# A four-layer convolution block on one core: the order of the start, of the spectra stage, of the attention weights, and fill products in the output stage

## The chip, the cores and the metric

The kernel runs on one core of a Trainium2 chip. The metric is device time in microseconds (us) of one execution. One profiled execution gives the trace that is read here; its rows give starts and durations, with the source line of the kernel.

The engines are TensorE (PE, with its weight loads shown apart as PEld), VectorE (DVE), ScalarE (ACT), GpSimd (POOL) and SyncE (SP), which issues most DMAs. [...]

## The reference, cut to what matters

Input x is (4, 56, 56, 128) in float32. Four layers follow each other, each with a residual and a group norm without weights in front of it:

```python
x = x + L0(_gn(x))   # shifted-window attention, global attention, MLP (per sample)
x = x + L1(_gn(x))   # all pairs of nodes in a row: relu(proj_i + proj_j), summed, then a linear
x = x + L2(_gn(x))   # spectral (FFT) convolutions, attention over the 56 images, two more spectral layers
x = x + L3(_gn(x))   # 3x1 convolution, sums over both axes, relu
```

In layer 2 each sample's 56 images are normalised, transformed by `rfft2`, multiplied by complex weights per head (32 heads) for K, Q and V, scored image against image, softmaxed, and mixed; then come projection, two spectral layers with norms, and the residuals.

## The kernel before, in words

All transforms are products with constant matrices. The stages, in order of time:

1. **Start** (to 48 us): `input_norms` loads the four samples and their norms, and computes a bound on the attention scores, which decides by a branch on the chip (`z_small`) whether the fast layers may be used. Python generators interleave the steps by hand: `norm_steps` for each sample, `products` (squared lengths) and `longest` (their maxima), `weights` (which runs `score_bounds`, `attention_bias` and `edge_weights`). `fill(n)` issues n products of ones whose result nobody reads.
2. **Layers 0 and 1** (48 to 2586.5 us): a loop over the four samples, `fast_layer` and then `edge_layer`. The normalised images of samples 0 to 2 (`xad`, and transposed `xat`) are written to DRAM by `normed_images` beside the next sample's work; sample 3 stays in `x1` in SBUF, and is normalised in the next stage.
3. **Spectra** (to 2671.3 us): `first_transform` (4 blocks `s_pr` of 28 products a sample, scaled by VectorE into `s_z` and copied by ScalarE) and `sample_spectra` (13 steps: three `s_ps`, two `s_pr2`, eight `s_px`, copied into S, iS, R and xh). `norm` is sample 3's `normed_images`, advanced by `go_on(n)`. Beside it POOL prepares the weights of the scores (`all_score_weights`) and of the values (`value_weights`, which ends in the DRAM tensor `dd`).
4. **Attention weights** (to 2801.6 us): `attention_weights` runs 72 items: for each of two pairs of samples (bp) and 16 columns c, one with n=0 (the operand `q_u` made by VectorE, 128x1792) and one with n=1 (made by POOL), and four odd ones per pair that read T and Tp. `make` issues an operand four items ahead, `product` the eight products of an item. `between` holds generators that get a step after each item: `skips`, and, when pair 0 is done, its `softmax`. `collect` adds a pair's sums.
5. **Attend** (to 3122.8 us): `attend` multiplies xh by `dd`'s values (VectorE `u_ud`, POOL `u_up`) and sums with the attention in `u_po`; pair 1's softmax is among its first steps.
6. **Outputs** (to the end): `outputs` records 788 operations in a `Plan`, and issues them in a fixed order, `OUTPUT_ORDER`. `bank` and `banks` hand out PSUM.

TensorE, ScalarE and VectorE run in the order of the program text in these stages (a manual schedule), POOL too from stage 4 on; SP's DMAs, and POOL's work before that, are placed by the framework's scheduler.

## Time and profile before

| | us |
|---|---|
| median of 3 runs | 3463.82 |
| lowest, highest | 3462.63, 3465.51 |
| profiled execution | 3464.84 |
| its span, first to last instruction | 3463.1 |

Busy time of the engines by stage, from one answer for these six stretches (us):

| stage | length | PE | DVE | ACT | POOL | mean granted clock |
|---|---|---|---|---|---|---|
| start | 48.0 | 27.28 | 29.72 | 16.32 | 7.95 | 0.92 |
| layers 0 and 1 | 2538.5 | 2460.57 | 1989.59 | 1862.21 | 648.89 | 1.00 |
| spectra | 84.8 | 77.21 | 39.98 | 32.72 | 39.72 | 0.96 |
| attention weights | 130.3 | 123.06 | 94.33 | 7.04 | 99.76 | 0.96 |
| attend | 321.2 | 316.49 | 277.84 | 68.49 | 267.01 | 0.99 |
| outputs | 340.2 | 314.41 | 226.41 | 144.36 | 222.59 | 0.98 |

The granted clock is TensorE's, as a share of full speed. A TensorE that is busy at half clock counts as busy, so the column PE and the clock are read together.

### The profile page before, as it was taken

Reading aid. Unit: us, or ns where it says so; the run is one execution under the profiler, and the core shown is the slowest. Engines: PE = TensorE matmul, PEld = TensorE weight load, DVE = VectorE, ACT = ScalarE, POOL = GpSimd, SP = SyncE. Lnnn points to the kernel's source line nnn. Section 1 sums busy time; section 2 is a strip of 40 time slices with the busy share of each in tenths; the row PEclk is TensorE's granted clock in tenths of the full one; section 3 lists DMA queues with packets and bytes.
Section 4 is the critical chain, followed back from the end, with each engine's and each line's share of the span. In section 5 each row is a group of like instructions: output and inputs, shape, how many; then the busy total and the mean of one; then the engine's idle time right before and its main releaser. Section 6 shows DMA issues by size and latency. Waiting matters only on the chain. (4 is left out here: it accounts for less than half of the span.)

```text
span 3463.1 us, 64456 instructions
## 1 busy us (share of the span) xinstructions
PE 3319.0 (96%) x27800; PEld 1425.6 (41%) x27800; DVE 2657.9 (77%) x2555; ACT 2131.1 (62%) x2253; POOL 1285.9 (37%) x796
## 2 busy tenths in 40 slices
PE   7999999999999999999999999999999999999998
PEld 4433333353333435333343443333337433336664
DVE  6588867867888696788859858887794778895776
ACT  4688876668888575788857668887653012215442
POOL 1000007800000491000019400000775778884786
PEclk9999999999999999999999999999999999999999
DMA  2143420024434000444310033442014037743101
GB/s 106 43 94 89 97 54 19 20 53 93 92 91 86 19 1 20 106 103 91 91 42 1 20 81 90 93 97 54 1 40 118 1 87 187 190 115 94 57 20 56
DMA packets 98012, 243.41 MB, mean 70 GB/s; under 512 B 64457, under 2 KB 69833, under 8 KB 92713
## 3 DMA queue, kind: packets, MB, share of 16 engines
q0 software_dynamic: 16128, 102.77, 14.8%
q1 hardware_dynamic: 74872, 123.61, 12.2%
q10 hardware_dynamic: 6720, 12.85, 1.3%
q8 instruction: 220, 3.60, 0.4%
q14 instruction: 72, 0.58, 0.1%
HBM read 79.43 MB, written 31.33 MB: 32 GB/s over the span
## 5 line engine op out<-in xcount | busy, mean ns | idle before, releaser
L830 ACT ACTIVATE f_ring<-f_pm 128x1792 f32<-128x1792 f32 (+1 forms) x764 | 1093.8, 1482 | 226.4 <-PE f_pm L827 179.6
L682 DVE TENSOR_TENSOR f_acc<-f_acc,f_ring 128x1792 f32<-128x1792 f32 x468 | 947.5, 2025 | 190.2 <-ACT f_ring L830 160.0
L827 PE MATMUL f_pm<-f_qT,f_kT 32*128 32x448 f32 x5376 | 722.6, 571 | 9.9 <-ACT f_p L716 4.1
L672 POOL DMA_DIRECT2D f_far<-f_ring x112 | 96.5, 862 | 1328.2 <-ACT f_ring L830 1033.4
L693 PE MATMUL f_pm<-f_ring,f_va 128*32 128x448 f32 (+1 forms) x6304 | 589.4, 490 | 0.0
L1269 POOL TENSOR_TENSOR e_tp<-e_a,e_c 128x1792 f32<-128x1792 f32 (+2 forms) x172 | 480.4, 2831 | 36.7 <-issue 36.7
L1267 DVE TENSOR_TENSOR e_td<-e_a,e_pc 128x1792 f32<-128x1792 f32 (+2 forms) x292 | 478.3, 1703 | 8.8 <-ACT e_c L1255 8.8
L827 PEld LDWEIGHTS f_pm<-f_qT,f_kT 32*128 32x128 f32 x5376 | 260.2, 183 | 411.5 <-ACT f_ring L830 300.3
L693 PEld LDWEIGHTS f_pm<-f_ring,f_va 128*32 128x32 f32 x6304 | 163.8, 109 | 410.1 <-issue 397.8
L1271 ACT ACTIVATE e_tp<-e_tp 128x1792 f32<-128x1792 f32 (+2 forms) x172 | 253.3, 1495 | 98.0 <-POOL e_tp L1269 98.0
L2018 DVE TENSOR_TENSOR u_ud<-u_px,u_d 112x1792 f32<-112x1792 f32 x144 | 263.4, 1863 | 39.7 <-PE u_po L2023 35.1
L2020 POOL TENSOR_TENSOR u_up<-xh,u_d 112x1792 f32<-112x1792 f32 (+1 forms) x72 | 240.9, 3373 | 55.0 <-PE u_po L2023 40.7
L1338 PE MATMUL e_acc<-e_td,t_edge 128*32 128x448 f32 x1952 | 231.6, 542 | 6.6 <-DVE e_td L1267 6.4
L2023 PE MATMUL u_po<-u_ud,AT 112*64 112x448 f32 x1056 | 213.9, 544 | 1.9 <-DVE u_ud L2018 1.9
L1338 PE MATMUL e_acc<-e_tp,t_edge 128*32 128x448 f32 x1184 | 147.9, 543 | 23.7 <-ACT e_tp L1271 23.7
L2023 PEld LDWEIGHTS u_po<-u_ud,AT 112*64 112x64 f32 x1056 | 74.3, 138 | 128.9 <-issue 112.8
L1338 PEld LDWEIGHTS e_acc<-e_td,t_edge 128*32 128x32 f32 x1952 | 61.6, 110 | 142.6 <-issue 93.7
L737 DVE RECIPROCAL f_den<-f_den 128x448 f32<-128x448 f32 x28 | 82.6, 2951 | 44.9 <-ACT f_den L734 44.9
L1862 POOL TENSOR_TENSOR q_u<-iS,q_g 128x1792 f32<-128x1792 f32 x32 | 102.8, 3235 | 22.8 <-PE q_acc L1877 22.8
L813 POOL TENSOR_TENSOR x<-xf,xw 128x343 f32<-128x343 f32 x28 | 25.5, 911 | 224.7 <-DVE xf L802 224.7
L1877 PE MATMUL q_acc<-q_u,S 64*64 64x448 f32 x1024 | 104.4, 552 | 4.4 <-DVE q_u L1864 3.3
L2121 ACT COPY x_ev<-x_po 56x896 f32<-56x896 f32 x32 | 28.8, 900 | 126.9 <-DMA x_xs<-xat 51.1
(525 smaller groups left out, 4579.1 us busy)
## 6 DMA issues: line engine op xcount, KB each, us to landing
f_far<-f_ring POOLq DMA_DIRECT2D x112, 896.0 KB, 6.4
u_d<-dd SPq DMA_DIRECT2D x46, 784.0 KB
f_far<-f_ring SPq DMA_DIRECT2D x28, 896.0 KB
xw<-in_x SPq DMA_DIRECT2D x4, 1568.0 KB
x2d<-x SPq DMA_DIRECT2D x4, 1568.0 KB
xat<-x SPq DMA_DIRECT2D x4, 1568.0 KB
x_xs<-xat ACTq DMA_DIRECT2D x32, 196.0 KB
xm<-x_ev ACTq DMA_DIRECT2D x64, 98.0 KB
```

Of the source, the lines that this page charges most:

```text
L682: nc.vector.tensor_add(e.acc, e.acc, slots(j, c))
L693: nc.tensor.matmul(e.po[heads[h], part], va[o, c, heads[h]], p, start=(c == 0), stop=(c == 23 and part.stop == NB))
L827: nc.tensor.matmul(ss[:, i, :NB], kT[heads[h], c * P:(c + 1) * P], qT[heads[h], blk(j)], start=True, stop=True)
L830: nc.scalar.activation(ring[:, slot:slot + m, :], ss[:, :m, :NB], AF.Exp, scale=scale)
L1267: nc.vector.tensor_tensor(t, am, cm, ALU.max)
L1269: nc.gpsimd.tensor_sub(t, am, cm)
L1271: nc.scalar.activation(tf, tf, AF.Relu)
L1338: nc.tensor.matmul(acc[quarters[r0 + r], :NB], w.S[:, 0, :], t[:, r].rearrange("p l n -> p (l n)"), start=(g == 0), stop=(g == len(turns) ...
L1877: nc.tensor.matmul(acc[bp][i][halves[hb % 2], hb // 2, :NB], x[o], u[o, 8 * hb:8 * hb + 8, :].rearrange("p h t -> p (h t)"), start=first, ...
L2018: nc.vector.tensor_mul(u, bc(px[:, :, :NB], 2, m), dm)
L2020: nc.gpsimd.tensor_mul(u, bc(x, 2, m), dm)
L2023: nc.tensor.matmul(po[64 * b2:64 * b2 + 64, :NB], st.AT[:, 8 * i + h0 + q, 2 * bp + b2, :], u[:, b2, q, :], start=(left == 16), stop=(left ...
```

## The change

- **Start.** The bias products and sums (`attention_bias`) go ahead of the last sample's norm; one fill of two is dropped; the lengths of sample 2 are reduced ahead of that sample's last norm step; the sums of the bounds go under the transpose of the maxima.
- **Spectra.** The buffer `xw` moves from the io pool to the right side of memory, and with one more row it also holds images. Image 0 is read into it (`first_image`) when the last sample's front has used it, so during the last edge layer; image 2 is read into it later; the images' pool has one buffer instead of two. All four transform blocks of sample 0 come first, and sample 3's statistics after them, four steps at a time in sample 0. Sample 3's normalisation itself is done by ScalarE instead of VectorE. The loads of the score and value weights, of `x2d` and of the convolution's weights are issued in a function `bulk` after the first transform, in that order.
- **Attention weights.** In pair 0 POOL's item of a column comes one column later; in pair 1 the generators get a step at every fourth item from item 42 on; four fills stand in front.
- **Attend.** Four fills stand in front, two behind the first head.
- **Outputs.** Eleven fills: seven into the PSUM that the operation at hand has just taken (`FILL_OWN`), four into an extra bank (`FILL_SPARE`).

On SP the order behind the last layer becomes: image 1 (two halves), qk4, qk, qkr, V, image 2's first half, Vrev, P, `x2d`, image 2's second half, `dd`, the eight convolution weights, four `apart`, two `u_d`, `xat`, four `apart`, Tp and T. On POOL the score weights come ahead of the value weights instead of mixed with them.

```diff
@@ input_norms
     longest(1)
-    fill(2)
-    next(steps[3])
+    fill(1)
     next(steps[3])
     products(2)
     longest(2)
+    next(steps[3])
     next(work)
     next(work)
     products(3)
-    next(work)
     longest(3)
...
-    for _ in range(2):
-        next(work)
+    next(work)
     nc.vector.tensor_reduce(k.longest, pt[0:1, :P], AX.X, ALU.max)
     fill(4)
@@ build, weights(ps)
-                    yield from score_bounds(k, w0, bounds, wk, ps)
+                    steps = score_bounds(k, w0, bounds, wk, ps)
+                    next(steps)
                     added = attention_bias(k, w0, wp)
+                    yield
+                    next(steps)
+                    added()
                     edge_weights(k, w1, wp)
                     yield
-                    added()
-                    yield
+                    yield from steps
@@ normed_images
+    if b == B - 1:
+        nc.vector.scalar_tensor_tensor(t1, mr[:, 0:1], -1.0, mr[:, 1:2], ALU.mult, ALU.mult)
...
         for t in range(0, HH, 14):
-            apply_norm(k, x[:, t:t + 14, :], x[:, t:t + 14, :], mr)
+            if b == B - 1:
+                nc.scalar.activation(x[:, t:t + 14, :], x[:, t:t + 14, :], AF.Identity, bias=t1, scale=mr[:, 1:2])
+            else:
+                apply_norm(k, x[:, t:t + 14, :], x[:, t:t + 14, :], mr)
@@ spectra
-        fill(3)
-        go_on(28)
-        next(first[0])
-        next(first[0])
-        go_on(1)
-        fill(4)
-        next(first[0])
-        go_on(1)
-        next(first[0])
-        go_on(2)
+        for n in range(4):
+            next(first[0])
+            if n == 2:
+                fill(4)
+        images(2)
+        bulk()
         for b in range(B):
             for n, _ in enumerate(sample_spectra(k, st, b, (wk, psum), zs.pop(b))):
-                go_on(2)
+                go_on(4 if b == 0 and n < 7 else 2 if b and n > 8 else 1)
@@ attention_weights
             for c in range(16):
-                seq += [(bp, c, 0, None), (bp, c, 1, None)]
+                seq.append((bp, c, 0, None))
+                if bp or c:
+                    seq.append((bp, c - (not bp), 1, None))
                 if c in (8, 10, 12, 14):
                     seq.insert(len(seq) - 1, (bp, None, c // 2 % 2, c // 12))
+            if not bp:
+                seq.append((bp, c, 1, None))
...
+        idle = psum.tile([P, 512], F32, tag="t", name="q_idle", bufs=1)
+        for _ in range(4):
+            nc.tensor.matmul(idle[:, :3 * P], k.ident, bc(k.ones, 1, 3), start=True, stop=True)
...
-            if n >= 3 and between and next(between[0], 0) == 0:
+            if n >= 3 and between and (item[0] == 0 or n % 4 == 2 and n > 38) and next(between[0], 0) == 0:
                 between.pop(0)
@@ attend
+        fill(4)
         prepare(0)
...
+                    if not turn and left == 15:
+                        fill(2)
@@ Plan, outputs
+FILL_OWN = {42: 1, 82: 1, 330: 1, 743: 2, 748: 2}
+FILL_SPARE = {30: 1, 160: 1, 273: 2}
...
+            if n in FILL_SPARE:
+                self.idle = FILL_SPARE[n]
...
+                self.spare()
+            self.idle = FILL_OWN.get(n, 0)
             op.run()
...
+        def filled(t, out):
+            for _ in range(plan.idle):
+                k.nc.tensor.matmul(out, k.ident, bc(k.ones, 1, 3), start=True, stop=True)
+            plan.idle = 0
+            return t
@@ build
+        xwp = x1s.enter_context(tc.tile_pool(name="xw", bufs=1, side="right"))
+        xi = xwp.tile([P, HH + 1, HH], F32, name="xw")
+        xw = xi[:, :HH, :].rearrange("p t h -> p (t h)")
...
-            xw = io.tile([P, TOK], F32, name="xw")
...
+            def first_image():
+                nc.sync.dma_start(xi[:, :HH, :], xad[0])
+                nc.gpsimd.memset(xi[:, HH, :], 0.0)
...
                 front(k, w0, xw, xf, x1, st)
+                if to is None:
+                    first_image()
                 edge_layer(k, w1, x1, st)
...
-        x2p = x2s.enter_context(tc.tile_pool(name="x2", bufs=2, side="right"))
+        x2p = x2s.enter_context(tc.tile_pool(name="x2", bufs=1, side="right"))
...
-        loaded = {}
-        for b in range(2):
-            images(b)
-        nc.sync.dma_start(x2d[B - 1], x1)
+        loaded = {0: xi}
+        images(1)
...
-                    all_score_weights(k, I, w2, sp, wk, st)
-                    value_weights(k, I, w2, wk, dd)
-                    spectra(k, w2, st, xat, images)
+                    def bulk():
+                        all_score_weights(k, I, w2, sp, wk, st)
+                        value_weights(k, I, w2, wk, dd)
+                        nc.sync.dma_start(x2d[B - 1], x1)
+                        load_weights(k, l3p, I, "w3_", w2)
+                        load_weights(k, l3p, I, "w2_", w2, only=CONV_WEIGHTS)
+
+                    spectra(k, w2, st, xat, images, bulk)
```

More of the change, by code (lines that the diff above doesn't have):

```diff
@@ L1649, in first_transform @@
     z = to[b] = wk.tile([P, 33, 2 * HH], F32, name="s_z")
-    xf = x.rearrange("p t h -> p (t h)")
+    xf = x().rearrange("p t h -> p (t h)")
     for t0 in range(0, HH, 14):
@@ L1696, in sample_spectra, with spectra @@
         yield
-def spectra(k, w, st, xat, images):
+def spectra(k, w, st, xat, images, bulk):
     nc, tc = k.nc, k.tc
@@ L1714, in spectra @@
         zs = {}
-        first = [first_transform(k, st, b, (wk, psum), st.x1 if b == B - 1 else images(b), zs) for b in range(B)]
+        first = [first_transform(k, st, b, (wk, psum), lambda b=b: st.x1 if b == B - 1 else images(b), zs)
+                 for b in range(B)]
         idle = tiny.tile([P, 512], F32, name="s_pt")
@@ L2005, in attend, with fill @@
         late = []
+        idle = bank()[:, 0, :3 * P]
+        def fill(n):
+            for _ in range(n):
+                nc.tensor.matmul(idle, k.ident, bc(k.ones, 1, 3), start=True, stop=True)
+        fill(4)
         prepare(0)
@@ L2175, in conv_weights @@
     yield
+FILL_OWN = {42: 1, 82: 1, 330: 1, 743: 2, 748: 2}
+FILL_SPARE = {30: 1, 160: 1, 273: 2}
 class Plan:
     def __init__(self, **buffers):
-        self.ops, self.buffers = [], buffers
+        self.ops, self.buffers, self.idle, self.spare = [], buffers, 0, None
     def add(self, engine, cost, run, after=(), takes=(), gives=(), lag=0.0, table=None):
@@ L2207, in issue @@
                 assert old < 0 or not users[b, taken[b][old]]
+            if n in FILL_SPARE:
+                self.idle = FILL_SPARE[n]
+                taken["b"].append(("idle", n))
+                users["b", ("idle", n)] = 0
+                old = len(taken["b"]) - 1 - self.buffers["b"]
+                assert not users["b", taken["b"][old]]
+                self.spare()
+            self.idle = FILL_OWN.get(n, 0)
             op.run()
@@ L2211, in issue @@
                 users[g] -= 1
+            assert not self.idle
 def half_sample(k, w, st, plan, b, half, whole, pools, rows, x2d, xm):
@@ L2775, in outputs @@
         opened, taken = [], [0]
+        def filled(t, out):
[3 more added lines that the diff above has]
+            return t
         def bank():
-            return psum.tile([P, 512], F32, tag="b", name="o_b")
+            t = psum.tile([P, 512], F32, tag="b", name="o_b")
+            return filled(t, t[:, :3 * P])
         def banks():
@@ L2782, in banks @@
             tag, bufs = ("x", 1) if taken[0] % 3 == 0 else ("px", 2)
-            return psum.tile([P, 2, 512], F32, tag=tag, name="o_d", bufs=bufs)
+            t = psum.tile([P, 2, 512], F32, tag=tag, name="o_d", bufs=bufs)
+            return filled(t, t[:, 0, :3 * P])
         pools.bank, pools.banks = bank, banks
@@ L2806, in outputs @@
                 p.after.append(op)
+        plan.spare = bank
         plan.issue([int(n) for n in OUTPUT_ORDER.split()])
@@ L2924, in build @@
                             pass
+                first_image()
         x2s = ExitStack()
-        x2p = x2s.enter_context(tc.tile_pool(name="x2", bufs=2, side="right"))
+        x2p = x2s.enter_context(tc.tile_pool(name="x2", bufs=1, side="right"))
         def images(b):
             if b not in loaded:
-                xp = loaded[b] = x2p.tile([P, HH + 1, HH], F32, name="s_x2")
+                xp = loaded[b] = xi if b == 2 else x2p.tile([P, HH + 1, HH], F32, name="s_x2")
                 for o in (slice(0, 29), slice(29, HH)):
                     nc.sync.dma_start(xp[:, o, :], xad[b, :, o, :])
-                nc.gpsimd.memset(xp[:, HH, :], 0.0)
+                if b < 2:
+                    nc.gpsimd.memset(xp[:, HH, :], 0.0)
             return loaded[b]
-        loaded = {}
-        for b in range(2):
-            images(b)
-        nc.sync.dma_start(x2d[B - 1], x1)
+        loaded = {0: xi}
+        images(1)
         l3p = es.enter_context(tc.tile_pool(name="l3", bufs=1))
-        load_weights(k, l3p, I, "w3_", w2)
-        load_weights(k, l3p, I, "w2_", w2, only=CONV_WEIGHTS)
         st.AbT = l3p.tile([P, 2, HH], F32, name="AbT")
```

## The prediction

> **What bounds the kernel now.** I read the page first: its busy row, the 40 slices, the chain that ended last. Then busy time and clock in stretches of a few microseconds around every stage that the diff touches, then the order of time and the releasers of TensorE in those stretches.

> ```profile
> PE 3319.0 (96%) x27800; PEld 1425.6 (41%) x27800; DVE 2657.9 (77%) x2555; ACT 2131.1 (62%) x2253; POOL 1285.9 (37%) x796
> ```

> TensorE is 96% busy. The four-sample main part (48 to 2586.5 us) is not edited in its work, so what can be won lies in the other 900 us, where TensorE waits or runs at a lower granted clock. The releasers of TensorE from 2585 to 2860 us (who was waited for, us in total, times, longest) name those waits:

> ```profile
> PE q_pt L1919 <- DVE y L1911: 5.9, 1, 5.9
> PE q_acc L1877 <- DVE q_u L1864: 3.3, 1, 3.3
> PE u_po L2023 <- POOL u_up L2020: 2.4, 1, 2.4
> PE u_po L2023 <- DVE u_ud L2018: 1.9, 1, 1.9
> ```

> Stretches of 5 us (length, then busy us and count of PE, PEld, DVE, ACT, POOL, then granted clock, DMA share, GB/s) show the clock: 1.00 is full, 0.50 half.

> ```profile
> 2605.00:2610.00 5.00, 3.54 (x61) 2.76 (x58) 2.73 (x10) 2.96 (x7) 2.31 (x8) 1.00 0.97 354
> 2610.00:2615.00 5.00, 5.00 (x68) 4.88 (x69) 1.36 (x3) 0.67 (x2) 4.90 (x9) 0.56 0.93 377
> 2615.00:2620.00 5.00, 5.00 (x78) 4.76 (x77) 3.60 (x3) 0.44 (x1) 4.90 (x9) 0.75 0.02 4
> ...
> 2670.00:2675.00 5.00, 3.72 (x24) 1.55 (x28) 5.00 (x3) 0.00 (x0) 5.00 (x3) 0.71 0.60 143
> ...
> 2745.00:2750.00 5.00, 2.98 (x16) 1.52 (x20) 4.97 (x4) 0.58 (x1) 1.01 (x1) 0.50 0.00 0
> ...
> 3415.00:3420.00 5.00, 5.00 (x10) 2.40 (x10) 4.41 (x6) 0.00 (x0) 4.92 (x4) 0.66 0.00 0
> ```

> So a busy TensorE ran at half clock from about 2610.2 to 2617.3, 2672 to 2675.5, 2747 to 2750.6, 2806 to 2812, 3399.2 to 3402.3 and 3415.6 to 3419.6 us; each loses half its length unless another engine is the limit there.

> **The change part by part.**

> *Start (0 to 48 us).* The bias products (16 records of `b_p`, 41.73 to 43.67) move ahead of the last sample's mean product, one fill goes, and the bounds' sums (`z_norm`, two reduces, 1.46 us) move behind the transpose of the maxima. Each fill is two records of about 0.33 us (0.65 us; twice that at half clock). Walked forward on the same rows: TensorE is free at about 31.75; `b_p` ends at 33.7; the mean product, one fill, the variance product end at 35.2 (34.0 before); the last sample's reciprocal now stands in VectorE's order behind the two maxima of sample 2 (free at 37.5, before 36.3), so the squares on ScalarE begin at 38.0 instead of 34.9 and end at 41.3; the lengths' products end at 42.3, the last maximum at 43.1, top and transpose 44.0. The 1.46 us of `z_norm` run from 43.3 beside the transpose, and `longest` starts at 44.9, where it starts now. So what the reorder takes from the tail it puts into the squares: 0 (bounds -0.7 to +1.0). But the four fills now follow the transpose at once:

> ```profile
> 44.71 5.28 PE L991 MATMUL z_p<-c_ones 128*1 128x384 f32 x8
> ...
> 50.11 0.50 PEld L375 LDWEIGHTS w_mm<-w_xg,t_first 128*128 128x128 f32 x2 [1.48 <-issue]
> ```

> Before, they run at half clock until 50.0 and hold up the first projection, whose input was ready at 48.1. From 44.0 they end at 46.6 (49.3 at half clock). Projection at 48.3: -1.8 us (-0.8 at half clock).

> *Spectra (2586.5 to 2671.3 us).* Image 0 is loaded into the new buffer during the last edge layer, whose stretch shows next to no DMA, and the last sample's 56 row statistics (6.71 us on VectorE, which hold back the first scalings `s_z` until 2596.5) go behind the first transform. TensorE's warm cost comes from rows: 56 records of a transform block take 1.76 us (2647.12 to 2648.88), a sample with four blocks 16.83 (2641.68 to 2658.51), the last sample 9.5 (2658.5 to 2668.0). Start after the branch stays at 2588.7, with 3 blocks 5.3, the four fills 2.7, a block 1.76, scaling and its latency 0.95: first `s_ps` at 2599.4 against 2602.08: -2.7. Sample 0 now lasts 22.35 us (to 2624.43), since it meets the half clock (3.6) and waits for statistics and DMA; streamed like sample 2 plus two small products it takes about 17.5: -4.8. Samples 0 and 1 carry the late statistics; I give back 0.4. Sum -7.1. The four normalisations of x move from VectorE (0.68 each at best) to ScalarE, where the nearest row is `o_sq`, 784 elements in 0.86: 3.4 us in one block late in sample 1. Behind it on ScalarE stand one copy of `s_px` and sample 2's copies; four banks of that tag cover 3.5 us of TensorE work, so 0 (up to +1.5).

> *Queues that are passed.* SP issues image 1, then qk4, qk, qkr, V, half of image 2, Vrev, P, `x2d`, the other half, `dd`, eight small weights, four `apart`, two `u_d`, `xat`, four `apart`, then T and Tp. Image 2's halves wait for transform 0 (2594 and 2598.5); with `x2d`, 3.2 MB at the 393 GB/s of 2590 to 2595 are down by 2608, and first use is in sample 1 near 2619. POOL's weight work starts 2.8 MB after 2587, at about 2595 instead of 2605.62, and takes the same 37.3 us: `dd` leaves at 2632 instead of 2642.95 and until then holds SP. Behind it wait the small weights (used much later), `apart` (needed through T at the first odd product, 34.7 us after the spectra end), and `xat` (read at 2829.5). All covered by 25 us or more: 0. If the cover were gone, each us late would be one on TensorE.

> *Attention weights (2671.3 to 2801.6 us).* The turn from batch pair 0 to 1 carries the largest wait:

> ```profile
> 2733.92 7.23 PE L1877 MATMUL q_acc<-q_u,S 64*64 64x448 f32 x64 [1.13 <-DVE y L1896]
> ...
> 2744.28 2.68 DVE L1911 TENSOR_TENSOR y<-y,q_den 128x896 f32<-128x896 f32 x1
> ...
> 2747.02 1.10 PE L1919 MATMUL q_pt<-t_shared,y 128*112 128x128 f32 x4 [5.88 <-DVE y L1911]
> ```

> From 2732.2 to 2756.0 TensorE does 7 items of 1.5 us and four transposes of 0.65, 13.3 us of work in 23.8. The change spreads the eight softmax steps over every fourth item of pair 1, so VectorE goes straight from the two collects (2.08) to the next `q_u`. I walked both orders through in-order engines with 2.02 (VectorE item), 3.19 (POOL), 1.5 and 1.66 (TensorE even, odd), 2.3 (skips): the 5.8 us wait goes, the 1.1 for the collect stays, and 1.2 us come back where the third item of pair 1 waits for VectorE. That is -4.2 from order, and the half clock (-1.9) and the stretched 2.68 us multiply (-1.6) go with it: -7.7. At the start, the gap of 3.3 us takes four fills (2.6 us), -1.2 if the clock then holds; TensorE meets VectorE's second item 0.5 us earlier than it is ready. POOL's products come one item later in pair 0, which only adds slack. Sum about -8, bounds -5 and -10.

> *Start of attend.* Six fills stand in front of and behind the first products. The clock was half here, but:

> ```profile
> 2812.66 3.90 DVE L2018 TENSOR_TENSOR u_ud<-u_px,u_d 112x1792 f32<-112x1792 f32 x2
> ...
> 2814.68 0.20 PEld L2023 LDWEIGHTS u_po<-u_ud,AT 112*64 112x64 f32 x4 [0.70 <-DVE u_ud L2018]
> ```

> At 2814.68 TensorE takes `u_ud` in the moment it is ready; VectorE, with the last softmax, sets the pace to there. A warm clock gains 0; fills that end at 2808.2 leave 1.2 us of slack. 0 (0 to +1).

> *Output stage.* Eleven fills of 0.65 us stand in gaps of TensorE of 0.66 to 1.34 us, so they cost 0 to 0.5 in all. Seven stand where the clock is 1.00 already. The last four fill two waits of 1.23 and 1.32 us before `o_d` L2683 (3414.9), whose first 13 records run at half clock and lie on the chain to the end: -2. The stretch at 3399 to 3402 is untouched. Sum -1.5.

> [...] The trace closes the gate at 3415.6, after waits of at most 1.3 us between very small products, and at 2610.2, where the stretch before it is 3.54 of 5 us busy and no wait is above 1.1. [...] By the rows, a stretch that is only half busy is enough, and -18.4 stands. I take the rows.

> **Sum**: -1.8 - 7.1 - 8.0 + 0 - 1.5 = -18.4 us. The profiled execution took 3464.84 us (span 3463.1), 1.0 above the median of 3463.82; so 3446.4 for it, 3445.4 for the median. I say 3445.5.

> **The rivals.**
> - *The clock is not held.* The gate still shuts in spectra (3.6), at the start of attention (1.2) and before the last products (2.0): 3452. For it: 2605 to 2610 was 70% busy and still led to half clock. Against: samples 1 to 3 streamed at 1.00. Chance 0.17.
> - *The gain in spectra is turned into a new wait*, and the start gives nothing: VectorE's statistics or ScalarE's normalisation hold the copies that TensorE needs. Then -18.4 + 7.1 + 1.8 = -9.5 and, with POOL (3.19 an item against TensorE's 3.0 a pair) pacing pair 1, about -6: 3458, no measurable change. Against: VectorE has about 12 us of work in sample 0's 17.5. Chance 0.05.
> - *Slower: SP's order.* `dd`, waiting for POOL, stands before `apart`. If POOL's work ended so late that T and Tp land more than 35 us after the spectra end, the odd products of pair 0 wait; from 53 us on the whole gain is gone and the time is above 3464, at 60 us about 3471. For it: SP waited 33.5 us for `d_f` in the trace. Against: the estimate has `dd` out 28 us before the spectra end. Chance 0.03.
> - *More than forecast*: attention at -10, spectra at -9: 3440, inside the range. Chance 0.1.

> **How the numbers follow.** The main case has 0.65 with 3441 to 3450. The range 3438 to 3455 takes in the better case and the clock that isn't held. This kernel's measurement tells about 0.2% (6.9 us) from no change; the main case, the clock case and the better one are all beyond it, so faster 0.92, same 0.05, slower 0.03.

> **What would show it.** Right: the first `s_ps` near 2.7 us sooner after the branch, clock 1.00 through spectra; spectra to the first `q_acc` about 7 us shorter; no transpose between the pairs, the wait of 5.9 gone and `q_acc` about 8 us shorter from first to last; the first 128x1792 `u_ud` to the end of attend unchanged; the first 18 `o_wr` products at full clock; the first projection near 48.3. Wrong: half clock in sample 0, waits of TensorE on `s_z` or `xh`, long waits of `q_acc` on POOL `q_u`, a wait on T.

## The result, and the profile after

The changed kernel took 3456.02 us (median of 14 runs, 3451.88 to 3460.26), the kernel before 3464.64 us (14 runs, 3461.41 to 3465.73). The ratio is 0.9975, with a 95% interval of 0.9968 to 0.9982: 8.6 us faster, where the prediction said 18.4. The profiled execution took 3455.78 us with a span of 3454.0, so it is an ordinary one of these.

The page's busy row of the changed kernel:

```profile
PE 3323.4 (96%) x27834; PEld 1429.7 (41%) x27834; DVE 2659.3 (77%) x2552; ACT 2134.5 (62%) x2257; POOL 1284.9 (37%) x795
```

TensorE has 34 records more (the fills), and the span is 9.1 us shorter. The waits of TensorE from 2585 to 2860 us in the changed kernel (who was waited for, us in total, times, longest):

```profile
PE s_pr L1658 <- issue: 3.7, 3, 1.6
PE x_po L2018 <- DVE y L1900: 2.2, 1, 2.2
PE q_acc L1881 <- DVE y L1900: 1.1, 1, 1.1
PE q_acc L1881 <- DVE q_u L1868: 0.9, 1, 0.9
```

The 5.9 us before the transposes of the pair turn are gone, and fills stand in the 3.3 us before the first items; the 0.9 us are at 2762.1, in front of an item of pair 1, where the prediction had given back 1.2. New is the first row: 3.7 us in three stops of `s_pr`, in front of which no engine and no transfer is named ("issue"). The first of them, 1.07 us, is the start of the stage (the kernel before waits 0.9 us there); the others, 1.6 and 1.06 us, lie inside rows of alike products. Stretches of the changed kernel (columns as in the prediction; the sixth number after the length, counts left out, is the granted clock):

```profile
2605.00:2610.00 5.00, 5.00 (x107) 4.32 (x104) 4.08 (x28) 2.40 (x6) 5.00 (x12) 1.00 0.36 142
2610.00:2615.00 5.00, 5.00 (x93) 4.84 (x92) 4.23 (x13) 1.94 (x4) 4.82 (x7) 1.00 0.01 3
2615.00:2620.00 5.00, 5.00 (x86) 4.77 (x85) 3.24 (x8) 1.82 (x6) 5.00 (x6) 1.00 0.01 3
...
2650.00:2655.00 5.00, 5.00 (x76) 4.76 (x76) 1.26 (x2) 1.04 (x3) 0.00 (x0) 0.71 0.83 114
2670.00:2675.00 5.00, 4.91 (x56) 2.15 (x52) 5.00 (x4) 0.00 (x0) 5.00 (x2) 1.00 0.06 16
2735.00:2740.00 5.00, 5.00 (x54) 2.49 (x50) 5.00 (x4) 2.23 (x2) 5.00 (x2) 1.00 0.00 0
...
3285.00:3290.00 5.00, 5.00 (x17) 2.70 (x16) 4.81 (x4) 1.04 (x2) 4.92 (x4) 0.50 0.72 143
...
3405.00:3410.00 5.00, 5.00 (x21) 2.97 (x20) 3.29 (x7) 0.17 (x1) 4.92 (x4) 1.00 0.00 0
```

The places of half clock that the prediction named (2610, 2672, 2745, 3415) run at 1.00 in this profile. But others have appeared where the clock had been full: in the spectra's last sample (2650), in the output stage (3285), and two windows in the layers (683 and 1957). The order of time at the start, first the branch's decision before, then the changed kernel:

```profile
46.52 0.14 DVE L1086 TENSOR_SCALAR z_small<-z_top 1x1 int32<-1x1 f32 x1
```

```profile
41.94 2.74 PE L991 MATMUL z_p<-c_ones 128*1 128x384 f32 x8
...
44.30 0.14 DVE L1084 TENSOR_SCALAR z_small<-z_top 1x1 int32<-1x1 f32 x1
...
46.00 0.30 PEld L375 LDWEIGHTS w_mm<-w_xg,t_first 128*128 128x128 f32 x2 [2.05 <-ACT w_xg L368]
```

The fills are done at 44.68, before the work behind the branch begins (45.20), and the first projection comes at 46.01 instead of 50.14. At the turn from pair 0 to pair 1, and at the first products of attend:

```profile
2730.51 17.79 PE L1881 MATMUL q_acc<-q_u,S 64*64 64x448 f32 x176 [1.13 <-DVE y L1900]
...
2733.30 1.08 DVE L1906 TENSOR_REDUCE q_red<-y 128x16 f32<-128x896 f32 x1
2734.41 1.09 DVE L1907 TENSOR_TENSOR y<-y,q_red 128x896 f32<-128x896 f32 x1
2735.42 7.81 DVE L1868 TENSOR_TENSOR q_u<-q_px,q_g 128x1792 f32<-128x1792 f32 x4
```

```profile
2797.04 2.02 DVE L2032 TENSOR_TENSOR u_ud<-u_px,u_d 112x1792 f32<-112x1792 f32 x1
2798.30 0.20 PEld L2037 LDWEIGHTS u_po<-u_ud,AT 112*64 112x64 f32 x4 [0.55 <-issue]
```

TensorE now streams 17.79 us of items without a transpose between them, and VectorE puts its softmax steps between the items in ones and twos.

**Where the time went.** Subtracting the two profiles would again take one execution for the program. The means below are of four profiles of the kernel before (the first, and e13 to e15) and three of the changed one (the first, e1 and e10). Mean length of each stretch, from the start of one product to the start of the next one named, in us:

| stretch | before, 4 profiles | changed, 3 profiles | difference | predicted |
|---|---|---|---|---|
| to the first `w_mm` | 49.85 (48.65 to 50.35) | 46.53 (46.01 to 47.07) | -3.3 | -1.8 |
| to the last `e_acc` (the layers) | 2536.48 (2533.60 to 2538.41) | 2538.57 (2537.79 to 2539.01) | +2.1 | 0 |
| to the first `s_ps` | 18.51 (18.35 to 18.67) | 18.50 (17.33 to 20.67) | 0.0 | -2.7 |
| to the last `s_px` | 63.42 (61.62 to 65.63) | 61.77 (60.90 to 63.33) | -1.7 | -4.4 |
| to the last `q_acc` | 132.36 | 124.84 | -7.5 | -8.0 |
| to the last `u_po` | 321.41 | 321.96 | +0.6 | 0 |
| to the end | 341.94 (340.83 to 343.43) | 341.59 (339.94 to 342.89) | -0.4 | -1.5 |
| sum | 3463.97 | 3453.76 | -10.2 | -18.4 |

So the attention weights gave what was forecast. The start gave more, but the layers took two thirds of it back; of the spectra's 7.1 us only 1.7 are there. And a mean of 45.2 us at half clock became 21.6 (the tail after the last product left out). At half speed that is worth at most 11.8 us, and not all of it counts: attend lost 4.8 us of its half clock and got no shorter.

### The profile page after: what moved, and what is told of

It reads as the page before. It is cut to its first block, busy times and chain, and to the rows that moved or that the text cites. A ratio compares the mean times of both kernels' runs of the same rounds, so it can differ in the third digit from the quotient of the medians.

```text
span 3454.0 us, 64520 instructions
## 1 busy us (share of the span) xinstructions
PE 3323.4 (96%) x27834; PEld 1429.7 (41%) x27834; DVE 2659.3 (77%) x2552; ACT 2134.5 (62%) x2257; POOL 1284.9 (37%) x795
## 5 line engine op out<-in xcount | busy, mean ns | idle before, releaser
L2034 POOL TENSOR_TENSOR u_up<-xh,u_d 112x1792 f32<-112x1792 f32 (+1 forms) x72 | 240.9, 3375 | 56.0 <-PE u_po L2037 42.7
L1336 PEld LDWEIGHTS e_acc<-e_td,t_edge 128*32 128x32 f32 x1952 | 61.7, 110 | 142.4 <-issue 94.0
L737 DVE RECIPROCAL f_den<-f_den 128x448 f32<-128x448 f32 x28 | 82.6, 2951 | 44.9 <-ACT f_den L734 44.9
L802 DVE SCALAR_TENSOR_TENSOR xf<-f_pm,t_first,xf 128x392 f32<-128x392 f32 x28 | 17.5, 626 | 113.3 <-PE f_pm L800 113.3
```

Source lines behind the costliest of these rows:

```text
L1336: nc.tensor.matmul(acc[quarters[r0 + r], :NB], w.S[:, 0, :], t[:, r].rearrange("p l n -> p (l n)"), start=(g == 0), stop=(g == len(turns) ...
L2034: nc.gpsimd.tensor_mul(u, bc(x, 2, m), dm)
```

## The experiments

**Once more (e1, e10).** Edit: none.

> The changed kernel once more, nothing edited, for a second profile. Theory A (the losses repeat): in the first profile VectorE's third input scaling at the start of samples 1, 2 and 3 took 3.61 us against 1.14 before, and TensorE came back 1.0 to 1.6 us late each time; if this is a fixed property of the program, the 3.61 stands again in all three samples, and so does the gap of about 1.6 us without a releaser in the third block of the first transform (2593.6 us). Theory B (chance): the 3.61, the gap, or the 10.24 us at half clock in the output stage are absent this time and the span differs by the difference, 2 to 10 us. Time by either: 3452 to 3460, 0.25% below the kernel before.

> The changed kernel a third time, beside the next one on the same chip. Theory (its level differs between calls through the clock alone): 3449 to 3457, and runs at mean granted clock 0.998 are 6 to 7 us below runs at 0.996. The scaling of 3.61 us stands in samples 1 to 3 once more if it is a property of this program.

e1: 3449.59 us (5 runs), ratio 0.9963 (0.9949 to 0.9976), below the 3452 to 3460 expected. e10: 3457.24 (13 runs), ratio 0.9977 (0.9969 to 0.9985), just above its 3449 to 3457. The changed program's level moves by nearly 8 us between one set of runs and another (the two intervals against before overlap), and the clock goes with it: over e10's 13 runs a mean granted clock lower by 0.001 goes with 2.4 us more (correlation -0.85), and e1's runs stood at 0.997 to 0.998, e10's at 0.994 to 0.997. The scaling of 3.61 us stands in all three samples of e1 and in two of e10 (1.14 in the other); the stop in the third block stands in both (1.74 and 1.72 us). The half clock of 10.24 us at 3284 is in neither. So the late scaling and the stop come back, and the half clock of the output stage was chance.

**The parts alone (e2 to e5)**: the hunks of one part in the kernel before, of which these are the cores.

```diff
 e2, start
-    fill(2)
-    next(steps[3])
+    fill(1)
...
+                    yield from steps
 e3, spectra
+        images(2)
+        bulk()
...
-                go_on(2)
+                go_on(4 if b == 0 and n < 7 else 2 if b and n > 8 else 1)
 e4, weights
-            if n >= 3 and between and next(between[0], 0) == 0:
+            if n >= 3 and between and (item[0] == 0 or n % 4 == 2 and n > 38) and next(between[0], 0) == 0:
 e5, fills of attend and outputs
+FILL_OWN = {42: 1, 82: 1, 330: 1, 743: 2, 748: 2}
+FILL_SPARE = {30: 1, 160: 1, 273: 2}
```

> The kernel before with the edits of the start alone (bias products among the lengths, bounds' sums under the transpose). The prediction's step: -1.8 us, all of it kept to the end. Theory A1 (the late scaling comes with the start's edit): first projection about 4 us earlier, and the 3.61 us scaling stands at samples 1 to 3, which takes 4 us back: 0 to +1 against before. Theory A2 (it comes with the input image's new place in memory, which this kernel does not have): the scaling stays at 1.14, and about -2.8 us is left at the end.

> The kernel before with the edits of the spectra alone, which include the input image's new place in memory and the loads moved behind the first transform. The prediction's step: -7.1 us. Theory A2 (late scaling comes with the new place): 3.61 us at samples 1 to 3 and TensorE about 1 to 1.6 us late each time, +4; the spectra give -3.3 as in the changed kernel, so about 0 in all. Theory A1 (it comes with the start's edit): scaling 1.14, layers unchanged, spectra -3.3 to -7.1. By either, first s_ps not earlier after the layers' end than in the changed kernel (16 us) if TensorE again stops in the third block for want of instructions.

> The kernel before with the edits of the attention weights alone (order of the items, softmax steps behind every fourth item, four fills). The prediction's step: -8.0 us (bounds -5 and -10), q_acc from first to last about 121 us against 129.5, and no other stretch changed, so the whole time about 8 us (0.23%) below before. Rival (the gain is partly a matter of where the half clock falls in the unchanged kernel): the stretch gives -4.2 from order alone and 3464.6 becomes about 3460.

> The kernel before with only the fills of attend and of the output stage. The prediction's step: 0 in attend, -1.5 in the output stage (clock full at the first o_wr products, half clock at 3399 untouched). Theory after the first profile: in the changed kernel neither half-clock stretch of the tail (3399, 3416) is left, so -3 to -3.5. Rival: the fills cost as much as they give, because stretches of small products elsewhere in the output stage still fall to half clock by chance: 0 +- 3, and the time spread is as wide as before.

| part alone | median, us (before 3463.2 to 3463.4) | ratio (95%) | predicted |
|---|---|---|---|
| e2 start | 3459.73 | 0.9990 (0.9982 to 0.9998) | -1.8 |
| e3 spectra | 3463.05 | 1.0003 (0.9995 to 1.0012) | -7.1 |
| e4 weights | 3460.05 | 0.9994 (0.9985 to 1.0003) | -8.0 |
| e5 fills | 3466.77 | 1.0009 (1.0000 to 1.0017) | -1.5 |

The parts don't add up to the whole: the four ratios give about 0.9996 together, the change 0.9975. In e3 TensorE stops in the third block of the first transform as in the changed kernel, for 1.68 us. The late scaling is bound neither to the start's edit (e2: 1.14 three times) nor to the input image's new place, for it stands in one sample of e3 and also in one of e4 and two of e5, which have neither; A1 and A2 both fall. In e5 the clock at the first `o_wr` products is full, but 17.1 us of half clock lie elsewhere in the output stage (from 3217, 3326 and 3401 us on), and the 3 to 3.5 us that were expected did not come: its rival, that the fills cost as much as they give, fits.

e4 held a surprise. From first to last `q_acc` it took 127.28 us instead of about 121: with the new order, but the old spectra before it, TensorE stops among the first skip products `q_pg`, and the clock falls behind it. This is e9, where the same happens (order of time, then two stretches, its own and the changed kernel's):

```profile
2677.06 1.55 PE L1890 MATMUL q_pg<-R 64*64 64x56 f32 x90
2682.02 0.90 PE L1890 MATMUL q_pg<-R 64*64 64x56 f32 x43 [3.41 <-issue]
```

```profile
2674.00:2678.00 4.00, 4.00 (x102) 2.50 (x99) 4.00 (x3) 0.00 (x0) 4.00 (x2) 1.00 0.89 201
```

```profile
2672.00:2676.00 4.00, 4.00 (x70) 2.12 (x66) 4.00 (x3) 0.00 (x0) 4.00 (x3) 1.00 0.02 4
```

The stop is inside one row of alike products, with nothing awaited. The trace has a DMA queue of kind "instruction" with pieces of 16384 bytes: 220 in a run, one for about every 255 records of TensorE (products and weight loads), so it is taken here as TensorE's code. In e9 one piece begins at 2679.28 and takes 1.31 us, and TensorE goes on at 2682.02. In the changed kernel the piece came at 2672.18, well ahead: the transfers into `u_d` were issued at 2635 there instead of 2671, and the DMA share at that time is 0.02 against 0.89.

The kernel before has these transfers at the same time, and no stop. There a piece begins at 2672.59, half a us ahead of their first large packet (2673.13); in e9 they begin at 2672.40 and the piece comes 6.9 us later. So the stop seems to take both: the transfers, and a piece that is needed while they run.

**Without the spectra's part (e9).** Edit: the changed kernel less e3's hunks.

> The changed kernel with the spectra as they were before (old order, loads and buffers); start, weights, attend and outputs changed. The prediction's step (-7.1 for the spectra): 7 us slower than the changed kernel of the same call. Theory from the stage lengths of the runs so far (old spectra without half clock 18.4 + 61.6 us, new 17.4 + 61.2): 1.0 to 1.5 us slower, plus 1.7 or 3.4 where the clock falls to half in the first sample. Rival: the old order of loads leaves a transfer beside the first skip products, where TensorE stopped 3.7 us for want of instructions in the run with the weights' edits alone; if that is what the early loads prevent, the stop stands again near 5.5 us after the first q_acc, and the kernel is 4 to 6 us slower.

3460.53 us (19 runs), 3.3 above e10 on the same chip, between the 1.0 to 1.5 of the theory and the 4 to 6 of the rival; ratio 0.9989 (0.9982 to 0.9996). Its attention weights took 126.70 us from first to last `q_acc`, against 121.18 in each of the changed kernel's profiles, with the stop of 3.41 us and one window of half clock behind it. By the stretches the spectra's edit is worth 1.8 us in the spectra themselves (80.36 us from the last `e_acc` to the last `s_px`, against 78.58 in e1, both without half clock) and 5.5 in the attention weights; the medians differ by less. The rival was right that it works in another stage. That it is the moved loads which keep this code piece early is the likeliest reading, since the stop stands in both profiles with the old loads and the new order (e4, e9) and in none of the eight with the new loads and the new order; no run moved one load alone.

**The late scaling, and the stop in the spectra (e6, e7, e8, e11).**

```diff
 e6, e8, e11
-            if g < 2:
+            if g < 3:
                 nc.scalar.activation(out, x, AF.Identity, bias=shift, scale=mr[:, 1:2])
 e7, e8, e11
-            if n == 2:
+            if n == 1:
                 fill(4)
```

> The changed kernel with the third group's input scaling moved from VectorE to ScalarE. Theory A (VectorE's operation that reads and writes on-chip memory is held until GpSimd's row of fills with zeros leaves a gap; the rows show it ending when they end): no VectorE scaling of 3.61 us is left in samples 1 to 3, the second projection comes 1.3 to 1.7 us earlier in each, the half clock at 683 and 1957 goes: -4 to -6 against the changed kernel. Theory B (the late projection has another cause, for instance ScalarE's own order): ScalarE gets 0.66 us more ahead of the first copies, and each sample starts later by up to 0.7: 0 to +3.

> The changed kernel with the spectra's four fills after the second block of the first transform instead of the third. Theory A (TensorE runs out of fetched instructions in the third block: a 16 KB piece of code lands at 2593.9 and TensorE goes on at 2595.2; four long fills are eight records and let the fetch catch up): the gap of 1.6 to 1.7 us in the third block goes, or moves to the fills with no loss, and first s_ps comes 1.0 to 1.7 us earlier after the layers' end; whole time -1 to -2. Theory B (the gap is a wait on data or memory): it stays in the third block with the same length, or becomes longer since the block starts later by 2.7 us: 0.

> The changed kernel with both edits, the third scaling on ScalarE and the fills after the second block. If both theories hold the gains add: -5 to -8 against the changed kernel on the same chip, and the prediction's 18 us against the kernel before is nearly reached (3445 to 3448). If only one holds, the gain is that one's.

> The changed kernel with the third scaling on ScalarE and the fills after the second block, beside the changed kernel on the same chip. By the stage lengths: layers 5.0 us shorter, spectra's start 0.9 shorter, so 5 to 6 us below the changed kernel. Rival (what is won early falls into half clock later): 0 to -2.

| | median, us | ratio to before (95%) | layers, us | last `e_acc` to first `s_ps`, us |
|---|---|---|---|---|
| e10, changed | 3457.24 | 0.9977 (0.9969 to 0.9985) | 2537.79 | 20.67 |
| e7 | 3453.62 | 0.9976 (0.9968 to 0.9983) | 2538.87 | 16.45 |
| e6 | 3450.62 | 0.9968 (0.9956 to 0.9980) | 2533.88 | 19.22 |
| e8 | 3449.96 | 0.9966 (0.9953 to 0.9978) | 2533.95 | 16.66 |
| e11 (as e8; with e10) | 3450.50 | 0.9967 (0.9957 to 0.9977) | 2533.94 | 16.45 |

The start of sample 1 in the changed kernel, order of time:

```profile
676.85 1.41 POOL L340 MEMSET w_qd<- 128x1568 f32 x1
677.33 3.61 DVE L193 TENSOR_SCALAR w_xg<-xw,mr 128x392 f32<-128x392 f32 x1
...
678.29 0.98 POOL L343 MEMSET w_vd<- 128x1056 f32 x1
...
679.26 1.41 POOL L340 MEMSET w_qd<- 128x1568 f32 x1
680.60 0.40 POOL L345 MEMSET w_vd<- 64x16 f32 x2
...
683.41 0.50 PEld L375 LDWEIGHTS w_mm<-w_xg,t_first 128*128 128x128 f32 x2 [2.98 <-ACT w_qd L223]
```

and in the kernel before:

```profile
679.67 1.41 POOL L340 MEMSET w_qd<- 128x1568 f32 x1
680.15 1.14 DVE L193 TENSOR_SCALAR w_xg<-xw,mr 128x392 f32<-128x392 f32 x1
...
681.01 0.33 POOL L341 MEMSET w_kT<- 128x16 f32 x1
681.06 0.30 POOL L342 MEMSET w_pT<- 128x16 f32 x1
681.11 1.15 POOL L343 MEMSET w_vd<- 128x1056 f32 x1
681.91 0.62 DVE L225 TENSOR_SCALAR w_qd<-w_mm,t_first 32x392 f32<-32x392 f32 x1 [0.62 <-PE w_mm L375]
...
684.48 0.30 PEld L375 LDWEIGHTS w_mm<-w_xg,t_first 128*128 128x128 f32 x2 [1.23 <-ACT w_qd L223]
```

A MEMSET is GpSimd's write of zeros. The scaling takes 0.48 us where GpSimd does not hold it (the median of this operation in the changed kernel); here it lasts as long as GpSimd's row of MEMSETs does. Before, it slips in after the first of them and ends at 681.3, and GpSimd's next one is 0.33 us long instead of 0.12. In the changed kernel seven MEMSETs follow each other from 676.85 to 680.72, and the scaling, begun at 677.33, ends at 680.94. The copy from PSUM at 681.91 is not held, though a MEMSET of 1.15 us runs beside it. TensorE's second projection waits for VectorE's copies behind the scaling: 2.98 us instead of 1.23. So the rows show each holding up the other: the scaling took 3.61 us beside a row of seven MEMSETs instead of 0.48, and a MEMSET behind a scaling 0.33 instead of 0.12. By what they do so, no run shows. With the scaling on ScalarE (e6, e8, e11, e12) the layers take 2533.9 to 2534.0 us, 4.6 us less than the changed kernel's mean, and neither a scaling of 3.61 nor half clock is left in them. This is e8:

```profile
676.95 1.92 ACT L368 ACTIVATE w_xg<-xw,shift,mr 128x392 f32<-128x392 f32 x3 [1.68 <-PE e_po L1283]
...
681.88 0.93 PE L375 MATMUL w_mm<-w_xg,t_first 128*128 128x392 f32 x2 [0.99 <-ACT w_qd L223]
```

Theory A of e6 stands for the layers. For the stop in the spectra, here the changed kernel and then e8:

```profile
2590.06 3.54 PE L1658 MATMUL s_pr<-t_images,xw 128*64 128x33 f32 x115 [1.07 <-issue]
2595.21 1.76 PE L1658 MATMUL s_pr<-t_images,xw 128*64 128x33 f32 x53 [1.61 <-issue]
2596.90 2.85 PE L1725 MATMUL s_pt<-c_ones,t_shared 128*128 128x384 f32 x8
2599.67 1.83 PE L1658 MATMUL s_pr<-t_images,xw 128*64 128x33 f32 x56
```

```profile
2585.80 3.46 PE L1658 MATMUL s_pr<-t_images,xw 128*64 128x33 f32 x112 [1.37 <-issue]
2589.18 1.24 PE L1725 MATMUL s_pt<-c_ones,t_shared 128*128 128x384 f32 x3
2591.00 1.88 PE L1725 MATMUL s_pt<-c_ones,t_shared 128*128 128x384 f32 x5 [0.58 <-issue]
2592.81 3.46 PE L1658 MATMUL s_pr<-t_images,xw 128*64 128x33 f32 x112
```

A block has 56 records, and the stop comes after 115, three into the third block, with every input at hand. A code piece begins at 2592.94 and takes 0.97 us; TensorE goes on at 2595.21. With the fills after the second block the stop comes in the fills and is 0.38 to 0.58 us in e7, e8 and e11; the first `s_ps` then is 16.45 to 16.66 us after the last `e_acc` instead of 17.33 and 17.51 (e10's 20.67 holds 6.8 us of half clock). But in e12, which has the same edit, the stop in the fills is 1.85 us and the first `s_ps` comes after 17.79: there the piece began 4.2 us after the stage's first product instead of 2.9 (e8). So the edit moves the stop, as theory A of e7 said, and gained 0.9 us in three profiles of four.

The reading that these stops are waits for code rests on more than one place. From 2580 to 2700 us the 18 profiles have 18 stops of over 0.3 us inside a row of alike products. Each ends 1.2 to 1.5 us after a code piece has landed (the end of its record), in the first transform, in the fills, in the last sample and among the skip products alike.

The whole time shows less than the stages. e11 is 6.7 us below e10 on the same chip by medians, and 14 us below the kernel before, but the two intervals against before overlap a little. On the other chip e6 (3450.62) and e8 (3449.96, where 3445 to 3448 was expected) are no faster than the unedited changed kernel in e1 (3449.59), and e7's ratio is the changed kernel's. So the 4.6 us are shown for the layers; what of them is left in the whole time was not settled.

**Without the output fills (e12).** Edit: e11 less the two tables of e5 and what uses them.

> The same as the one before without the eleven fills of the output stage. The prediction's step: 1.5 us slower. Theory from the profiles so far (output stage 340.7 to 343.7 us without the fills, 339.9 to 345.7 with them): no difference that can be told, 0 +- 2. Rival (fills shut half clock out of the tail): 3.4 us slower, with the clock at half near the first o_wr products again.

3455.31 us by the median (3447.43 to 3467.70, 14 runs), but 0.9969 (0.9959 to 0.9979) by the ratio, against e11's 3450.50 and 0.9967. In the profiles the output stage took 346.78 us with 20.5 us at half clock here, and 341.96 with 10.2 in e11. With the spread of single runs at 20 us this tells nothing certain of the fills.

**Further profiles of the kernel before (e13 to e15) and of the start alone (e16).** Edit: none, or e2's.

> The kernel before, nothing edited, a second profile. Two terms of the prediction took what one profile showed for a property of the program: VectorE's third scaling at 1.14 us in samples 1 to 3 (so that the layers cost nothing), and 6.83 us of half clock in the first sample of the spectra (worth 3.6). Theory A (properties of the program): both stand again. Theory B (each execution draws them anew: [...] the half clock by where the grid of 3.41 us lies): in three looks the scaling is 3.61 at least once in nine, and the half clock is absent from the first sample of the spectra at least once, where first s_ps to last s_px is then 61.3 to 61.7 us against 65.63.

> The kernel before, nothing edited, a third profile; expected as for the second. If the stretch from first s_ps to last s_px is 61.5 us without half clock and 63.2 or 65 with one or two grid windows of it, all of its variation is the clock.

> The kernel before, nothing edited, a fourth profile; expected as for the second. Attention weights: half clock at the pair turn (near 2744 us) in every profile, since VectorE lets TensorE idle there whatever the grid, and first to last q_acc 129 to 131 us.

> The start's edits alone, a second profile. In its first the scaling was 1.14 us in all three samples and the kernel gained what the start gave. If the edit of the start sets the odds of the late scaling, some of 3.61 us show here; if not, 1.14 stands in all three, and the layers take 2533.6 to 2535.1 us.

| kernel before | third scaling in samples 1, 2, 3, us | layers, us | first `s_ps` to last `s_px`, us | of it at half clock |
|---|---|---|---|---|
| the profile of the prediction | 1.14, 1.14, 1.14 | 2533.60 | 65.63 | 6.8 |
| e13 | 3.61, 1.14, 3.61 | 2535.77 | 64.73 | 6.8 |
| e14 | 3.61, 1.14, 3.61 | 2538.41 | 61.62 | 0 |
| e15 | 3.61, 3.61, 3.61 | 2538.14 | 61.69 | 0 |

Theory B holds for both: the scaling is held in 7 of 12 sample starts of the kernel before (11 of 12 in e1, e7, e10 and the first profile of the changed one, 3 of 3 in e9, 4 of 9 in e3 to e5, 1 of 6 in e2 and e16), and the half clock of sample 0 is there in two profiles of four. Half clock at the pair turn of the attention weights was no such draw: it stands in all four, 6.8 or 10.2 us, as e15 expected (from first to last `q_acc` 127.53 to 130.52 us, a little wider than its 129 to 131). The profile from which the prediction was made was the best of four for the layers and the worst for the spectra. What shifts the odds of the hold between kernels stays open.

## Why the prediction was wrong, point by point

In the means the gain is 8.2 us short of the forecast: 5.4 are missing in the spectra, 2.1 in the layers, 2.2 in the last three stages together, and the start gave 1.5 more. The step that failed is the spectra's sum; the other is a term that was put at nothing, the layers.

- **Start, -1.8.** The fills' term was right: from `z_small` to the first projection 3.6 us became 1.7. "What the reorder takes from the tail it puts into the squares: 0 (bounds -0.7 to +1.0)" was wrong: the squares began at 36.4, not at 38.0, the reduce into `longest` at 42.7, not at 44.9, and `z_small` came 2.2 us earlier. The measured -3.3 in the means is better than forecast.
- **Layers, no term at all.** The sum began by saying that the main part is not edited in its work. It isn't, but each sample starts with the race of VectorE and GpSimd shown above. The first projection's lead of 4.1 us in the pair of profiles was 2.8 after the fourth scaling of sample 0 (held 2.63 us), and then 1.2, 0.5 and -1.2 after the starts of samples 1 to 3: a hold costs 0.7 us, and 1.6 where a window of half clock follows it (683 and 1957). In the means the layers cost 2.1; the old ones run from 2533.60 to 2538.41, so part of this may be a draw too.
- **Spectra, -7.1: the step that failed.** The term -4.8 was "Sample 0 now lasts 22.35 us (to 2624.43), since it meets the half clock (3.6) and waits for statistics and DMA". The 3.6 was that execution's draw: without half clock the old spectra take 61.62 and 61.69 us from first `s_ps` to last `s_px`, the new ones 61.07 and 60.90 (61.30 in e3 and e6), so streaming is worth 0.3 to 0.8 where 4.8 were forecast. The term -2.7 for the first `s_ps` lacked the stop that is read here as a wait for code, 1.6 to 1.7 us in the third block, and 1.1 of the 2.7 was left (17.4 against 18.5). Half clock then came in the new one too, behind such stops: at 2649.5 in the first profile, behind that of 1.06 us, and for 6.8 us in e10, behind that of 1.72; the same stop in e1 is not followed by any.
- **Attention weights, -8.** Right: from first to last `q_acc` 129.55 us became 121.18, and it is 121.17 to 121.19 in all eight profiles that have the new order and the new spectra, while the old order varied from 127.5 to 130.9. What was not seen: it needs the new spectra before it (e4, e9). (The 13.3 us of work that the prediction gives TensorE there are 13.1 by its own figures; nothing hangs on it.)
- **Attend, 0.** Right: 321.40 us to 321.64 in the pair, and 0.6 more in the mean from one window of half clock in e10, at 2793.9, in the fills that stand there to hold the clock. The half clock that fell away had cost nothing, as forecast.
- **Outputs, -1.5.** The clock at the first `o_wr` products was full, as forecast. But the half clock came back at 3284, 10.24 us, and the means differ by 0.4. "Seven stand where the clock is 1.00 already" was again read from one execution; e12 could not settle whether the eleven fills do anything.
- **The rows' half-busy stretch.** The prediction took from its rows that a half-busy stretch is enough to lose the clock. In kind the runs bear this out: where few columns passed (under 2000 in 3.41 us), half clock followed on 56 of 114 windows in which TensorE was busy for at most 3.35 us, and on 3 of 50 in which it was busy for longer. But in the first profile the clock was held at the places that the prediction named, and the loss was elsewhere. What the prediction did not ask is where the grid lies (last section).
- **Queues passed, 0.** No wait on data that was moved. That moving the loads also seems to make way for a piece of code (e9) was not seen.

The second rival (3458), in which the spectra gain nothing, came nearest in time to the 3456.02 measured. It was right that the spectra's gain would be missing, but not in why: the longest wait of TensorE on VectorE or ScalarE in the spectra is 0.7 us, and the start gave more, not nothing. The first, "the clock is not held" (3452), named the wrong windows: those three were held in the profile, and others fell.

## What to carry to other kernels

A profile shows one draw of everything that hangs on a race or on the clock's grid, so take at least three before a term of a few us is read from a stretch of half clock or from an operation of unlike lengths. Hold GpSimd's rows of MEMSETs against VectorE's operations beside them: here a scaling beside a row of seven took 3.61 us instead of 0.48, and moving one scaling to ScalarE made the layers 4.6 us shorter. Look for a code piece ahead of a stop marked "issue" inside a row of alike small products: here there was one each time. Moving four long products to that place gained 0.9 us in three profiles of four, and with the big loads gone from it the stop among the skip products did not come.

## What the runs showed of the hardware that had not been expected

```profile
3282.00:3284.00 2.00, 2.00 (x19) 1.96 (x19) 1.40 (x5) 1.98 (x3) 2.00 (x2) 1.00 0.04 8
...
3286.00:3288.00 2.00, 2.00 (x6) 0.83 (x8) 2.00 (x4) 0.90 (x2) 2.00 (x2) 0.50 1.17 217
```

```profile
3292.00:3294.00 2.00, 2.00 (x19) 1.96 (x18) 1.40 (x4) 1.98 (x3) 2.00 (x2) 1.00 0.00 0
...
3296.00:3298.00 2.00, 2.00 (x15) 1.14 (x12) 2.00 (x4) 0.67 (x2) 2.00 (x2) 1.00 1.27 249
```

- It is the grid that differs. These products stand in all 18 profiles. In two the grid cut them so that one window held 1521 or 1514 columns (the changed kernel's first profile and e11), and both times 10.24 us of half clock followed; in the other sixteen no window there held fewer than 1749, and none followed.
- Counted over all grid windows of the 18 profiles that were themselves at full clock, from 48 us to the last product (columns by the records' starts), half clock followed on all 23 windows under 1400 columns, on 16 of 22 with 1400 to 1600, on 15 of 55 with 1600 to 1800, on 5 of 64 with 1800 to 2000, and on 28 of some 17,600 above. Columns are not the whole of it: under 2000 columns the clock fell behind 3 of 50 windows in which TensorE was busy for over 3.35 us, and behind 56 of 114 in which it was not. So a stage with few columns per window falls or not by where the grid lies; what exactly is weighed stays open. That this makes most of the spread from run to run is likely, from the clock that goes with each time, but was not tried by itself.
- Code pieces of 16384 bytes take 0.9 to 1.8 us each, and TensorE stood still for 1.6 to 1.7 us (first transform), up to 1.3 us (last sample) and 3.4 to 3.7 us (skip products) inside rows of small products, until 1.2 to 1.5 us after such a piece had landed.
